# A reordered schedule: lora products paired by batch, gates mixed in eight array tiles

## The chip, the cores and the metric

The kernel runs on one core of a Trainium2 chip. The metric is the time of the device in microseconds (us), as the median of several runs; one further execution is taken by the profiler, and all durations below come from it. The core has a matrix engine TensorE (PE), whose weight loads run beside it (PEld), the vector engine VectorE (DVE), ScalarE (ACT), GpSimd (POOL), and SyncE (SP), which here only issues DMAs. Each engine works off its own queue in order and waits for others through semaphores.

## The reference

```python
# x (64, 64, 1024) is N, C, L; every product is float32
y = conv1d(x, cond_weight, kernel 9, pad 4, 4 groups of 16 channels)
y = y + (cond_128 @ c_weight.T)[:, :, None] + fside_S_0[None, :, None]
# the ffn sees y as 8 batches of 512 rows of 1024
base  = y @ kernel + bias                              # kernel 1024 x 1024
A_eff = einsum('bn,nri->bri', gate, lora_A)            # gate 8 x 16: each batch's mixture
B_eff = einsum('bn,nor->bor', gate, lora_B)            # rank 32
delta = einsum('bor,btr->bto', B_eff, einsum('bri,bti->btr', A_eff, y))
delta = delta + (y @ lora_A_shared.T) @ lora_B_shared.T
out   = x + base + delta
```

## The kernel before

Float32 products are made of three products of rounded parts: each operand is split into a high part (a cast on ACT, steps whose names end in `hi`) and a rest (a subtraction on DVE or POOL, names ending in `lo`), and high times high, high times low and low times high are added in PSUM. The subtraction of step `xlo`, `ylo`, `wlo` and so on runs on DVE where the step ends in `v` and on POOL where it ends in `p`.

The 64 samples are 32 tiles of two; a pair `p` is two such tiles, so there are 16 pairs, and a batch `b` of the ffn is the two pairs 2b and 2b+1. For each pair and each of the four channel groups `g` an input is loaded (`xload`), split, and convolved. For pairs 3 to 15 the convolution is done in a difference form: `xdiff`, `xohi`/`xolo`, `xdhi`/`xdlo`, then `convo` (three matmuls) and `convd` (six); `evmid` and `evac` bring the sums out of PSUM and add the condition, and `turned` transposes the tile into `z`. The 1024 x 1024 product is done by a seven-product scheme (`prod p j`, twelve matmuls each) with sums of input blocks made on POOL (`asum`), splits `yhi`/`ylo`, copies `keep`, and additions `xsum`, `ysum`, `radd`, `yadd`, `total`; pair 0 alone is done plainly (`plain`). The shared lora is folded into the weights at the start (`fmm`, `fadd`).

The lora of each batch works so. `gmask` makes a tile `gm` of gates laid out for a product; `mix w j` multiplies it with raw loads `ls` of lora A (w = 0) and B (w = 1); `mixout` copies the result out of PSUM (ACT), `mixput` writes it to a buffer `eff` in DRAM, and `aload b` and `bload b h` read one batch's part back. `lora p` multiplies A of the batch with pair p's `z` in four tiles of the array of 128 rows by 32 columns; `axlow`, `axsum`, `axhi`, `axlo` add and split the result; `delta p b` multiplies it with B and adds it into the accumulator, and only then `total` may read it.

The order of all work is a text, `ORDER`, a list of about 1,840 steps that was written out beforehand. The program runs the steps in this order, and every engine, queues of DMAs included, keeps it for its own instructions:

```python
    for step in ORDER.replace("\n", " ").split(","):
        if step.strip():
            name, *args = step.split()
            steps[name](*(int(a) if a.isdigit() else a for a in args))
```

So a step's place in the text decides what it waits behind. Accumulators take one of five PSUM banks (`pmm`), convolutions one of two (`pcv`), the lora product has one (`axp`, two halves by p % 2). SP issues the loads and the writes to `eff`; ACT's queue issues the first small loads and the stores. At the start 29 matmuls on a constant tile (`warm`, `busy 29`) run until the first data are there.

Of the kernel before, what the change touches and what calls it, by code (L numbers as in the profile page):

```python
# [10 lines left out]
ALU = mybir.AluOpType  # L11
# [39 lines left out]
small 1, warm, twload 1, busy 29, twload 0, cwload, gload, ctload, cwide, cmul, thi 2, small 0, thi 0, tlo 0 v,  # L51
xload 0 0, xhi 0 0, tlo 2 p, xload 0 1, xlo 0 0 v, conv 0 0, twsum v, xhi 0 1, xlo 0 1 v, conv 0 1, sbload 1,
sbhi 1, csum, evac 0 0 v, turned 0 0, xload 0 2, xhi 0 2, xload 0 3, saload 0, sblo 1 p, xlo 0 2 p, evac 0 1 v,
turned 0 1, saload 1, gmask, xhi 0 3, conv 0 2, xlo 0 3 p, sahi 1, conv 0 3, sahi 0, salo 0 v, fmm 0 1,
sbload 0, sbhi 0, fmm 1 1, wload 1 0, evac 0 2 a, xload 1 0, sblo 0 v, fmm 1 0, salo 1 v, xload 1 1, xhi 1 0,
xhi 1 1, xlo 1 1 p, xlo 1 0 v, turned 0 2, yhi 0 0, ylo 0 0 p, wload 0 1, fadd 0 1, evac 0 3 a, fadd 1 0,
conv 1 0, whi 7 0, fmm 4 0, turned 0 3, xload 1 2, xhi 1 2, wlo 7 0 v, fmm 3 0, wload 1 1, conv 1 1, fadd 1 1,
wload 4 0, fmm 0 0, whi 0 1, wload 0 0, fadd 0 0, evac 1 0 a, plain 0 1 0, fadd 4 0, xlo 1 2 p, turned 1 0,
whi 0 0, wlo 0 1 p, fmm 2 1, fmm 2 0, yhi 0 7, evac 1 1 a, conv 1 2, fmm 5 0, wload 2 1, wload 2 0, fadd 2 0,
wlo 0 0 p, plain 0 0 0, xload 1 3, fadd 2 1, wload 5 0, xhi 1 3, fmm 4 1, xlo 1 3 p, plain 0 0 1, whi 0 2,  # L60
ylo 0 7 v, fadd 5 0, plain 0 3 0, whi 7 1, yhi 0 4, wload 3 0, fadd 3 0, whi 0 3, wload 5 1, fmm 3 1, conv 1 3,
turned 1 1, wlo 7 1 v, wload 3 1, xload 2 0, plain 0 1 1, fadd 3 1, whi 7 2, evac 1 2 v, wlo 7 2 p, wload 4 1,
wlo 0 3 p, wlo 0 2 v, lload 0 6, plain 0 2 0, whi 7 3, plain 0 3 1, fadd 4 1, wload 7 1, turned 1 2, whi 1 1,
plain 0 1 2, lload 0 7, xhi 2 0, plain 0 0 2, ylo 0 4 v, plain 0 3 2, xlo 2 0 v, plain 0 2 1, fmm 5 1,
evac 1 3 a, xload 3 0, wlo 7 3 v, plain 0 2 2, turned 1 3, whi 1 0, yhi 0 1, ylo 0 1 v, fadd 5 1, whi 6 1,
conv 2 0, wload 7 0, thi 1, xdiff 3 0 0 v, wload 6 0, evac 2 0 a, lload 1 5, wlo 1 0 p, fmm 7 0, fadd 7 0,
plain 0 2 3, plain 0 0 3, fmm 6 0, lload 0 2, plain 0 3 3, plain 0 1 3, fadd 6 0, lload 0 5, whi 6 0, asum 1 2,
yhi 1 2, lload 0 0, yhi 1 0, plain 0 0 4, plain 0 2 4, wsum 2 2 v, whi 2 2, lload 1 1, wlo 1 1 p, plain 0 0 5,
fmm 6 1, tlo 1 v, plain 0 2 5, rload 0 2, wlo 6 0 v, wsum 2 1 v, wsum 2 3 v, whi 1 2, wlo 1 2 v, plain 0 1 4,
whi 2 1, asum 1 3, whi 1 3, wlo 1 3 p, xload 2 2, wload 6 1, fadd 6 1, xload 2 1, whi 6 2, lload 0 1, xhi 2 2,  # L70
plain 0 3 4, lload 0 4, plain 0 2 6, lload 1 0, lload 0 3, wsum 2 0 v, fmm 7 1, plain 0 2 7, xload 2 3,
plain 0 0 6, fadd 7 1, whi 6 3, total 0 2, lload 1 6, mix 0 0, mixout 0 0 a, wlo 6 2 v, xhi 2 1, wlo 6 3 v,
wlo 6 1 v, wsum 3 2 v, xlo 2 2 v, mix 0 3, mixout 0 3 a, mix 0 2, mixout 0 2 a, wsum 3 0 v, wsum 5 0 v,
mixput 0 0, whi 2 3, mix 0 1, wsum 3 1 v, mix 1 0, mixput 0 3, mixout 0 1 a, xdiff 3 0 1 p, wsum 4 0 v,
conv 2 2, wlo 2 2 v, whi 2 0, wlo 2 0 v, ylo 1 2 v, plain 0 1 5, wsum 5 1 v, rload 0 0, wsum 5 2 v, wsum 4 2 v,
xlo 2 1 v, plain 0 0 7, mixput 0 1, ylo 1 0 p, mixput 0 2, wlo 2 1 v, prod 1 0, plain 0 1 6, wsum 3 3 v,
wsum 5 3 v, rload 0 1, plain 0 3 5, wsum 4 3 v, bihi, whi 3 2, keep 1 0, plain 0 1 7, lload 1 3, wsum 4 1 v,
plain 0 3 6, mixout 1 0 a, lload 1 7, mix 1 3, aload 0, whi 5 3, yhi 1 3, rload 0 3, lload 1 2, ylo 1 3 v,
mixout 1 3 a, total 0 1, lora 0, mix 1 1, turned 2 0, lora 1, whi 5 0, bilo, xohi 3 0, lload 1 4, mix 1 2,
whi 4 2, wlo 4 2 v, mixout 1 1 a, xolo 3 0 v, whi 3 0, wlo 3 0 v, wlo 3 2 v, yhi 1 1, ylo 1 1 v, mixout 1 2 a,  # L80
asum 1 5, total 0 0, whi 4 1, conv 2 1, axlow 1, axsum 1, xload 3 2, wlo 4 1 p, wlo 2 3 v, whi 4 0,
plain 0 3 7, axlow 0, axsum 0, mixput 1 0, mixput 1 3, wlo 4 0 v, xhi 2 3, xlo 2 3 v, wlo 5 3 v, axhi 1,
prod 1 1, biput 0, axlo 1, whi 3 3, asum 1 6, yhi 1 6, wlo 3 3 v, mixput 1 1, evac 2 1 a, turned 2 1, aload 1,
mixput 1 2, total 0 3, evac 2 2 v, turned 2 2, bload 0 0, whi 3 1, axhi 0, prod 1 2, keep 1 2, conv 2 3,
bhi 0 0, biput 1, yhi 2 0, evac 2 3 a, blo 0 0 v, axlo 0, yhi 1 4, bload 0 1, wlo 3 1 p, prod 1 3, ylo 2 0 v,
delta 0 0 1, total 0 0 1, bhi 0 1, blo 0 1 v, ylo 1 6 p, prod 1 6, whi 4 3, delta 0 3 1, wlo 4 3 v, store 0 0,
ylo 1 4 p, turned 2 3, delta 0 2 1, total 0 3 1, xdhi 3 0, convo 3 0, yhi 1 5, whi 5 1, ylo 1 5 v, xdlo 3 0 v,
delta 1 0, total 0 2 1, xload 3 1, keep 1 3, prod 1 4, evmid 3 0 a, store 0 3, xohi 3 1, xdiff 3 1 0 v,
xdiff 3 1 1 p, wlo 5 1 p, delta 0 1 1, total 0 1 1, wlo 5 0 v, xolo 3 1 p, convd 3 0, evac 3 0, turned 3 0,
asum 2 3, rload 1 0, convo 3 1, yhi 2 1, xdhi 3 1, xdlo 3 1 v, prod 2 0, whi 5 2, store 0 2, delta 1 2,  # L90
xload 3 3, keep 2 0, wlo 5 2 p, yhi 2 3, prod 1 5, total 1 0, xohi 3 3, xolo 3 3 v, asum 2 2, xdiff 3 2 0 p,
store 1 0, convo 3 3, evmid 3 1 a, xdiff 3 2 1 p, convd 3 1, ylo 2 3 v, prod 2 3, rload 1 3, delta 1 1,
ylo 2 1 v, xsum 1, asum 2 5, prod 2 1, xdhi 3 2, evac 3 1, turned 3 1, rload 1 2, radd 1 2 v, xdlo 3 2 v,
xdiff 3 3 0 v, delta 1 3, xohi 3 2, xdiff 3 3 1 p, yhi 2 5, xolo 3 2 v, ylo 2 5 p, yhi 2 2, ylo 2 2 v,
evmid 3 3 a, radd 1 3 v, convo 3 2, total 1 2, store 0 1, evmid 3 2 a, convd 3 2, xdhi 3 3, xdlo 3 3 v,
rload 1 1, radd 1 1 v, bload 1 0, lora 2, axlow 2, asum 2 6, prod 2 2, total 1 1, convd 3 3, evac 3 2,
turned 3 2, axsum 2, xload 4 0, xohi 4 0, xolo 4 0 p, bhi 1 0, yhi 2 4, ylo 2 4 v, axhi 2, prod 2 5, keep 2 3,
yhi 3 0, ysum 1 p, xdiff 4 0 0 v, xdiff 4 0 1 v, prod 2 4, store 1 1, xload 4 1, xohi 4 1, xolo 4 1 p,
yadd 1 v, blo 1 0 v, xdhi 4 0, axlo 2, delta 2 0, yhi 2 6, evac 3 3, keep 2 2, xdlo 4 0 v, convo 4 0,
turned 3 3, convd 4 0, rload 2 0, evmid 4 0 a, total 1 3, total 2 0, ylo 3 0 v, lora 3, xdiff 4 1 0 v,  # L100
xdiff 4 1 1 p, asum 3 3, yhi 3 3, prod 3 0, convo 4 1, ylo 3 3 v, evac 4 0, turned 4 0, xdhi 4 1, xload 4 3,
xohi 4 3, xdlo 4 1 v, asum 3 2, xolo 4 3 v, yhi 3 2, ylo 2 6 v, xload 4 2, xdiff 4 2 0 p, store 1 2,
xdiff 4 2 1 p, xohi 4 2, prod 3 3, yhi 3 1, bload 1 1, evmid 4 1 a, delta 2 2, ylo 3 2 v, xolo 4 2 v, asum 3 5,
store 2 0, convd 4 1, xdhi 4 2, xsum 2, convo 4 2, evmid 4 2 a, evac 4 1, xdlo 4 2 v, rload 2 2, radd 2 2 p,
total 2 2, xdiff 4 3 0 v, xdiff 4 3 1 p, prod 2 6, turned 4 1, yhi 3 4, bhi 1 1, convd 4 2, evac 4 2, keep 3 0,
prod 3 2, ylo 3 1 v, rload 2 3, radd 2 3 v, ysum 2 v, convo 4 3, yadd 2 v, xdhi 4 3, xdlo 4 3 v, ylo 3 4 v,
aload 2, prod 3 1, convd 4 3, turned 4 2, blo 1 1 p, xload 5 0, yhi 3 5, xohi 5 0, keep 3 2, asum 3 6,
keep 3 3, xload 5 1, xohi 5 1, delta 2 3, prod 3 4, delta 2 1, xdiff 5 0 0 p, xdiff 5 0 1 v, axlow 3,
ylo 3 5 p, evmid 4 3 a, total 2 3, prod 3 5, store 2 3, xolo 5 0 p, rload 2 1, yhi 3 6, radd 2 1 p, rload 3 0,
axsum 3, evac 4 3, axhi 3, turned 4 3, yhi 4 0, axlo 3, delta 3 0, xload 5 2, xdhi 5 0, store 1 3, xdlo 5 0 v,  # L110
convd 5 0, convo 5 0, ylo 3 6 v, bload 2 0, ylo 4 0 v, xdiff 5 1 0 v, xdiff 5 1 1 p, total 2 1, prod 3 6,
evmid 5 0 a, prod 4 0, asum 4 3, yhi 4 3, evac 5 0, xsum 3, yhi 4 4, ylo 4 3 p, delta 3 3, delta 3 2,
total 3 0, ylo 4 4 v, lora 4, xolo 5 1 p, xdhi 5 1, xdlo 5 1 v, store 3 0, yhi 4 1, ylo 4 1 v, xohi 5 2,
convo 5 1, keep 4 0, bhi 2 0, prod 4 1, rload 3 3, asum 4 2, yhi 4 2, radd 3 3 v, turned 5 0, xdiff 5 2 0 p,
ysum 3 v, evmid 5 1 a, xdiff 5 2 1 v, ylo 4 2 v, delta 3 1, xolo 5 2 p, rload 3 1, radd 3 1 p, blo 2 0 v,
# [702 lines left out]
```

## Time and profile before

| | before |
|---|---|
| median of 3 runs | 448.08 us (446.77 to 449.16) |
| profiled execution, its time | 447.48 us |
| its span | 445.7 us |
| PE busy | 438.3 us, 98% |
| DVE busy | 391.3 us, 88% |
| ACT busy | 251.2 us, 56% |
| POOL busy | 234.5 us, 53% |
| DMA | 67.05 MB, 150 GB/s on average |

Busy time of an engine is the time in which at least one of its instructions runs; an instruction that overlaps the one before it counts only with what it adds. The chain of waits is followed back from the last instruction, at each step to what released it. A group of the page is all instructions of one source line, engine and operation with the same tiles, with the mean duration of one in ns and the idle time of the engine before them. Matmuls are pipelined, so their durations overlap; start to start is what one costs.

### The profile page before, as it was taken

The numbers are of one execution on the slowest core, as the hardware profiler recorded it, in microseconds if no ns is written. First come the engines' busy times: TensorE is split into PE (matmuls) and PEld (weight loads), VectorE is DVE, ScalarE is ACT, GpSimd is POOL, SyncE is SP. The second block draws the span as 40 slices with busy tenths as digits, with TensorE's granted clock in tenths as the row PEclk, the third lists the DMA queues.
The fourth block names the chain that finished last, engine by engine and source line by source line (L and its number), as shares of the span: only waits on it lengthen the run. The fifth ranks groups of instructions, "written<-read, shape, count | busy, mean of one in ns | idle before, by whom it ended". The sixth has DMA issues, their size and how long they took to land.

```text
span 445.7 us, 7717 instructions
## 1 busy us (share of the span) xinstructions
PE 438.3 (98%) x2557; PEld 358.7 (80%) x2557; DVE 391.3 (88%) x615; ACT 251.2 (56%) x639; POOL 234.5 (53%) x202
## 2 busy tenths in 40 slices
PE   8999999999999999999999999999999999999996
PEld 7677658888888888888878888888888888888884
DVE  5998979899899899889899899899798989887783
ACT  5877468556655566446555655646554745654440
POOL 3766024754747653555444445464656475467543
PEclk9999999999999999999999999999999999999999
DMA  8999582461625463534345453443536354262243
GB/s 229 300 280 308 147 251 66 142 186 49 186 82 158 136 190 110 170 120 136 97 139 147 151 182 91 119 142 90 175 98 186 95 169 151 72 222 90 91 150 118
DMA packets 52488, 67.05 MB, mean 150 GB/s; under 512 B 6112, under 2 KB 34016, under 8 KB 52448
## 3 DMA queue, kind: packets, MB, share of 16 engines
q1 hardware_dynamic: 42512, 49.83, 38.9%
q10 hardware_dynamic: 9936, 16.73, 10.2%
q8 instruction: 20, 0.33, 0.3%
q14 instruction: 20, 0.16, 0.1%
HBM read 47.65 MB, written 18.87 MB: 149 GB/s over the span
## 4 chain that ended last, share of the span: by engine, by line
PE 91%; DMA 4%; DVE 2%; issue 1%; SPq 0%; ACT 0%; ACTq 0%; DVEq 0%
PE mm_a L592 19%; PE mm_d L592 18%; PE mm_c L592 17%; PE mm_b L592 9%; PE cv L346 8%; PE cm L346 4%; PE axp L602 3%; PE cv L318 2%; DMA wr<-in_dram 2%; PE mx L528 2%; PE mm_a L580 1%; PE mm_c L580 1%; DMA ls<-in_dram 1%; DMA ctt<-in_dram 1%; PE mm_d L580 1%; PE mm_a L660 1%
## 5 line engine op out<-in xcount | busy, mean ns | idle before, releaser
L592 PE MATMUL mm_a<-wh,y 128*128 128x512 f32 x240 | 79.6, 392 | 0.0
L592 PE MATMUL mm_d<-wh,y 128*128 128x512 f32 x240 | 79.2, 391 | 0.0
L592 PE MATMUL mm_c<-wh,y 128*128 128x512 f32 x240 | 79.1, 391 | 0.0
L364 ACT ACTIVATE md<-cm,cadd 128x64 f32<-128x64 f32 x208 | 48.2, 315 | 44.8 <-PE cm L346 41.1
L326 POOL TENSOR_TENSOR xf<-xt 128x256 f32<-128x256 f32 x45 | 33.3, 747 | 49.4 <-DVE xd L270 39.4
L265 ACT CAST xd<-xf 128x512 fp32r<-128x512 f32 x52 | 32.5, 626 | 44.9 <-PE cv L346 20.7
L265 ACT CAST y<-s 128x512 fp32r<-128x512 f32 x60 | 37.2, 624 | 30.5 <-POOL s L412 15.3
L592 PEld LDWEIGHTS mm_a<-wh,y 128*128 128x128 f32 x240 | 45.1, 188 | 9.9 <-issue 0.4
L592 PEld LDWEIGHTS mm_d<-wh,y 128*128 128x128 f32 x240 | 45.1, 188 | 9.2 <-issue 0.2
L592 PEld LDWEIGHTS mm_c<-wh,y 128*128 128x128 f32 x240 | 45.1, 188 | 9.1 <-ACT c L636 0.2
L387 DVE STREAM_TRANSPOSE z<-v 128x512 f32<-128x512 f32 x64 | 45.4, 709 | 3.2 <-PE axp L602 1.9
L592 PE MATMUL mm_a<-wl,y 128*128 128x512 f32 x120 | 46.9, 391 | 0.0
L592 PE MATMUL mm_c<-wl,y 128*128 128x512 f32 x120 | 46.8, 390 | 0.0
L592 PE MATMUL mm_d<-wl,y 128*128 128x512 f32 x120 | 46.8, 390 | 0.0
L346 PE MATMUL cv<-xd,th 128*128 128x256 f32 x208 | 45.7, 282 | 0.4 <-DVE xd L270 0.4
L378 DVE TENSOR_TENSOR v<-cv,md 128x512 f32<-128x512 f32 x52 | 35.7, 686 | 7.7 <-PE cv L346 2.5
L270 DVE TENSOR_TENSOR xd<-xf,xd 128x512 fp32r<-128x512 f32 x41 | 34.5, 842 | 7.6 <-ACT xd L265 7.4
L270 DVE TENSOR_TENSOR y<-s,y 128x512 fp32r<-128x512 f32 x49 | 38.2, 782 | 3.0 <-ACT y L265 2.7
L592 PE MATMUL mm_b<-wh,y 128*128 128x512 f32 x120 | 39.6, 391 | 0.0
L346 PEld LDWEIGHTS cv<-xd,th 128*128 128x128 f32 x208 | 35.5, 188 | 2.4 <-DVE xd L270 0.6
L265 ACT CAST y<-z 128x512 fp32r<-128x512 f32 x49 | 30.6, 625 | 11.8 <-DVE c L641 4.5
L326 DVE TENSOR_TENSOR xf<-xt 128x256 f32<-128x256 f32 x59 | 33.7, 587 | 0.2
(132 smaller groups left out, 1008.2 us busy)
## 6 DMA issues: line engine op xcount, KB each, us to landing
xt<-in_dram SPq DMA_DIRECT2D x64, 258.0 KB, 3.2
r<-in_dram SPq DMA_DIRECT2D x64, 256.0 KB, 3.5
out_dram<-r ACTq DMA_DIRECT2D x63, 256.0 KB, 2.6
ls<-in_dram SPq DMA_DIRECT2D x16, 256.0 KB, 4.6
br<-eff SPq DMA_DIRECT2D x48, 64.0 KB, 2.8
wr<-in_dram SPq DMA_DIRECT2D x16, 176.0 KB, 4.2
eff<-ls SPq DMA_DIRECT2D x16, 128.0 KB, 2.7
wr<-in_dram SPq DMA_DIRECT2D x16, 80.0 KB, 3.9
```

The source lines that it names most:

```text
L265: nc.scalar.copy(dst, src)
L270: engs[eng].tensor_tensor(dst, src, f32(hi), ALU.subtract)
L318: nc.tensor.matmul(ps, a[:, 2 * kt, g, :], b[:, :, kt:kt + P], start=(n == 0), stop=(n == 5))
L326: engs[eng].tensor_tensor(xdf[p, g][:, e], m, odd(p, g), ALU.subtract)
L346: nc.tensor.matmul(ps, a[:, w, g, :], b, start=(n == 0), stop=(n == 2))
L364: nc.scalar.activation(t[:, n], cpm[p, g][:, n], ACTF.Identity, bias=c[:, n:n + 1])
L378: nc.vector.tensor_tensor(v.rearrange("p n (i e) -> p e n i", e=2), cps.pop((p, g)), mid.pop((p, g)).unsqueeze(1).to_broadcast([P, 2, 4, H ...
L387: nc.vector.transpose(z[:, :, :, :, gg, :], vs.pop((p, g)).rearrange("p m j -> p (m j)"))
L528: nc.tensor.matmul(mps[w, j][n * e:n * e + n], gm.rearrange("p b i -> p (b i)"), lraw[w, 2 * j + e], start=True, stop=True)
L580: nc.tensor.matmul(acc[p, BLOCKS[b]], m[:, kk, :], n, start=(k == 0 and q == 0), stop=(k == 7 and q == 2))
L592: nc.tensor.matmul(ps, a[:, k, :], b[bb, k], start=s, stop=(k == HK - 1 and q == 2), skip_group_check=not first)
L602: nc.tensor.matmul(axp[q * R:q * R + R, p % 2, :], a[:, k, :], zs[p, hf][:, k, :], start=k < 2, stop=k >= 6)
```

## The change

Three things change. The lora products of the two pairs of a batch are issued one behind the other by a new step `loras b` (for b = 1 to 7; the first batch keeps two single steps). The gates are mixed in tiles of 64 rows by 32 columns of the array, eight at a time, in four calls instead of eight; gate mask, PSUM tiles, `eff` and the DMAs to and from it are laid out to match. And the whole order is written anew, with other choices of engine for some steps and, as the change puts it, with late DMAs allowed for. The number of `mixout` copies, of DMAs and their sizes stays.

The functions, in full:

```diff
-    NC = P // GC
-    eff = [dram.tile([NC, NB * GC, AW], F32, tag=f"eff{w}", name=f"eff{w}") for w in range(2)]
+    HI = GC // 2
+    eff = [dram.tile([4, NB, 2, 2, 2, HI, AW], F32, tag=f"eff{w}", name=f"eff{w}") for w in range(2)]
     gg = const.tile([P, NB], F32, name="gg")
-    gm = const.tile([P, NB, GC], F32, name="gm")
+    gm = const.tile([P, NB, HI], F32, name="gm")
...
     def gmask():
         ident = slot("s", "ident", (P, P))
         make_identity(nc, ident)
-        mask = slot("s", "mask", (P, GC))
-        nc.vector.tensor_reduce(mask, ident.rearrange("p (i n) -> p i n", i=GC), AX.X, ALU.add)
-        nc.vector.tensor_tensor(gm, gg.unsqueeze(2).to_broadcast([P, NB, GC]),
-                                mask.unsqueeze(1).to_broadcast([P, NB, GC]), ALU.mult)
+        mask = slot("s", "mask", (P, HI))
+        nc.vector.tensor_reduce(mask, ident.rearrange("p (r i n) -> p i r n", r=2, i=HI), AX.XY, ALU.add)
+        nc.vector.tensor_tensor(gm, gg.unsqueeze(2).to_broadcast([P, NB, HI]),
+                                mask.unsqueeze(1).to_broadcast([P, NB, HI]), ALU.mult)
...
     def mix(w, j, pool="m"):
         pl, tag = {"m": (pmm, "mm"), "c": (pcv, "cv")}[pool]
-        mps[w, j] = pl.tile([P, 2 * AW], F32, tag=tag, name=f"mx{w}_{j}")
-        n = NB * GC
-        for e in range(2):
-            nc.tensor.matmul(mps[w, j][n * e:n * e + n], gm.rearrange("p b i -> p (b i)"), lraw[w, 2 * j + e],
-                             start=True, stop=True)
+        for r in range(2):
+            mps[w, j, r] = pl.tile([P, 2 * AW], F32, tag=tag, name=f"mx{w}_{j}_{r}")
+        n, m = NB * HI, P // 2
+        for e in range(4):
+            for r in range(2):
+                nc.tensor.matmul(mps[w, j, r][n * e:n * e + n], gm[m * r:m * r + m].rearrange("p b i -> p (b i)"),
+                                 lraw[w, 2 * e + j][m * r:m * r + m], start=True, stop=True)
...
-    def mixput(w, j):
-        n = NB * GC
-        for e in range(2):
-            dst = eff[w].rearrange("c p a -> p c a")[:, 4 * j + 2 * e:4 * j + 2 * e + 2, :]
-            nc.sync.dma_start(dst, mev[w, j][n * e:n * e + n].rearrange("p (c a) -> p c a", c=2))
+    def mixput(w, j, r):
+        for c in range(2):
+            dst = eff[w][:, :, j, c, r].rearrange("e b i a -> (e b) i a")
+            nc.sync.dma_start(dst, mev[w, j, r][:, c * AW:c * AW + AW])
...
+    def loras(b):
+        for p in range(BP * b, BP * b + BP):
+            lora(p)
```

The order, its beginning, one stretch from the middle with a `loras`, and its end:

```diff
-small 1, warm, twload 1, busy 29, twload 0, cwload, gload, ctload, cwide, cmul, thi 2, small 0, thi 0, tlo 0 v,
-xload 0 0, xhi 0 0, tlo 2 p, xload 0 1, xlo 0 0 v, conv 0 0, twsum v, xhi 0 1, xlo 0 1 v, conv 0 1, sbload 1,
...
+gload, sbload 1, cwload, gmask, small 0, sbhi 1, twload 0, warm, twload 1, sblo 1 v, xload 0 0, busy 29, xload 0 1,
+cwide, sbload 0, ctload, cmul, thi 2, saload 0, tlo 2 v, twsum p, xload 0 2, thi 0, tlo 0 v, xhi 0 0, xhi 0 1,
+saload 1, xlo 0 0 v, xload 1 0, xload 0 3, wload 0 0, conv 0 0, xlo 0 1 v, sbhi 0, sblo 0 v, sahi 0, wload 3 0,
...
+yhi 6 6, xsum 6, asum 7 3, keep 6 3, xolo 8 1 p, keep 7 0, keep 6 2, ysum 6 v, xload 8 2, evmid 8 0 a,
+ylo 6 4 v, convd 8 0, bhi 3 1, loras 3, axlow 6, axsum 6, yhi 7 3, ylo 6 6 p, blo 3 1 v, convo 8 1, prod 7 1,
+ylo 7 3 v, xload 8 3, xohi 8 3, axhi 6, asum 7 2, axlo 6, prod 6 6, evac 8 0, xdhi 8 1, xdlo 8 1 p, yhi 7 4,
...
+radd 15 3 v, delta 15 1, yadd 15 v, total 15 3, radd 15 1 v, rload 15 0, delta 15 0, store 15 3, total 15 0,
+store 15 0, rload 15 2, radd 15 2 v, delta 15 2, total 15 2, ylo 15 6 p, prod 15 6, totalh 15 1 1, store 15 2,
+totalh 15 1 0, storeh 15 1 0, storeh 15 1 1
```

Steps that change their engine, over the whole order (the letter at the end of the step): from ACT to DVE 14 of the 52 `evmid` and one `evac`; from POOL to DVE five `radd`, seven `wlo`, five `blo`; from DVE to POOL ten `xdiff`, three `ylo`, two `ysum`, one `yadd`, two `wsum`, one `xdlo`, one `xolo` and two of the first splits.

## The prediction

> **What bounds the kernel now.** I read the busy shares of the page first, then the shares of the chain of waits.
>
> ```profile
> PE 438.3 (98%) x2557; PEld 358.7 (80%) x2557; DVE 391.3 (88%) x615; ACT 251.2 (56%) x639; POOL 234.5 (53%) x202
> PE 91%; DMA 4%; DVE 2%; issue 1%; SPq 0%; ACT 0%; ACTq 0%; DVEq 0%
> ```
>
> TensorE (PE) sets the end; VectorE (DVE) is the only other engine near it. So three things count: how much PE work goes, when PE starts, and whether DVE, ten points behind, still delivers in time. For the first I read the pieces of the chain in order of time around one lora product, and the groups of the two products that change.
>
> ```profile
> 291.88 0.70 PE cv L346 x6
> 292.58 1.01 PE axp L602 x32
> 293.60 2.97 PE mm_a L592 x12
> ...
> L528 PE MATMUL mx<-ls,gm 128*64 128x512 f32 x32 | 9.0, 610 | 0.5 <-DMA ls<-in_dram 0.4
> L602 PE MATMUL axp<-z,ar 128*32 128x128 f32 x512 | 17.3, 276 | 0.0
> ```
>
> To see: a lora product holds PE for 1.01 us, and the product behind it takes 2.97 where its like take 2.72 to 2.76. For the start I read the timeline of the first microseconds and, later on, of the gate tile.
>
> ```profile
> 0.86 0.27 DVE L695 MEMSET axt<- 98x256 f32 x1 [0.86 <-PEq L806]
> 1.18 5.38 PE L701 MATMUL idle<-axt 98*128 98x256 f32 x29 [1.18 <-DVE axt L695]
> 1.67 0.45 ACTq L506 DMA_DIRECT2D gg<-in_dram  x1
> 7.47 0.48 PE L318 MATMUL cv<-xsh,th 128*128 128x512 f32 x1
> ...
> 12.43 0.99 DVE L513 TENSOR_TENSOR gm<-gg,mask 128x64 f32<-128x64 f32 x1
> ```
>
> To see: the 29 idle matmuls start as soon as DVE has written their operand, at 1.18, and end 0.9 us before the first convolution. Last, DVE's busy time in stretches of 25 us, and what it waited for in the first 135 us.
>
> ```profile
> core 0: us, PE busy (x) PEld busy (x) DVE busy (x) ACT busy (x) POOL busy (x), PEclk, DMA share, GB/s
> 0.00:25.00 25.00, 22.54 (x100) 17.35 (x101) 19.86 (x32) 17.61 (x39) 14.00 (x17) 1.00 0.92 264
> 25.00:50.00 25.00, 25.00 (x109) 17.59 (x108) 23.75 (x37) 17.48 (x37) 12.46 (x10) 1.00 0.84 255
> 50.00:75.00 25.00, 24.55 (x157) 17.26 (x156) 21.75 (x39) 15.87 (x37) 6.82 (x5) 1.00 0.63 176
> 75.00:100.00 25.00, 24.99 (x150) 20.77 (x149) 22.15 (x31) 14.37 (x39) 15.59 (x13) 1.00 0.50 156
> 100.00:125.00 25.00, 25.00 (x155) 21.16 (x154) 23.29 (x38) 14.25 (x37) 14.08 (x13) 1.00 0.40 119
> ...
> DVE cwe L727 <- DMA cwt<-in_dram: 3.7, 1, 3.7
> DVE z L387 <- PE axp L602: 1.9, 1, 1.9
> DVE r L666 <- PE dl L660: 1.4, 2, 1.0
> ```
>
> To see: DVE's idle time in the first 125 us is 14.2 us, 5.1 of it before 25 us.
>
> **The change part by part.** Clock of the sum: the profiled execution took 447.48 us (span 445.7); the median of the runs is 448.08, so 0.6 goes on top of what comes out.
>
> *Lora products.* From two runs per batch to one, for batches 1 to 7; batch 0 keeps two. Inside a run the 32 matmuls come as eight groups of four, a group every 0.109 us: 0.87. A run costs 1.01 plus 0.22 on what follows (2.97 less 2.75), so entering and leaving costs 0.36. Seven pairs of switches go: -2.5 us of PE. The trace shows no lora directly behind a lora; if the second had to wait for the first, nothing would be saved, so between 0 and -2.5, and I take -2.5 because groups inside a run pay nothing. What waits longer: every delta of the earlier pair, and with it its accumulators in PSUM (five banks). The order puts one to three products between loras and its first delta (2.7 us each, against about 2.5 for the chain axlow, axsum, axhi, axlo by their rows), so nothing is added, except at most 0.5 at loras 5 and 7, where one product alone covers.
>
> *Gate mix.* Before, 8 calls of two 128x64 tiles; now 4 calls of eight tiles of 64 rows by 32 columns. The eight calls held PE for 8.9 us, of which 1.2 and 0.4 at 57 to 61 us were waits for the ls loads; a clean call is 0.93 (4.67 for five in the chain). A matmul is 0.44 from start to start on its tile and goes in two passes, so eight tiles side by side need 0.9 to 1.0 a call: 4.0 for four, against 7.4. Since each call now stands alone among full-array products, some three more switches at 0.3: net -2.5, and the waits (-1.6) may go or come again. Side by side by columns is shown by the lora row (four tiles start within 0.02 us); by rows nothing is shown. The Trainium skill ("TensorEngine Tiling (Array Packing)", Key Properties and Gotcha 1) says that tiles run independently, but that row tiles must not be in one PSUM bank at once. The code gives the two row halves different banks, so the rule allows -2.5; but a call then takes two of the five banks at once, a cost that the rule names and the old row does not have. If the halves ran one after the other, each call would double: +1.2 instead of -2.5. I take -2.5 and keep +1.2. mixout stays eight ACT copies (0.59 each), mixput 16 DMAs of 128 KB, aload and bload the same count and bytes with rows of 1 KB as before: nothing, covered by the several microseconds between landing and use; without that cover, one 3.3 us load once.
>
> *The head.* gmask now stands before warm in DVE's queue, and its product needs the gate load. That load is now first on ACT's queue, at about 0.74; the load that held this place (bia) landed after 3.3 us and the gate itself took 3.7, so it lands at 4.0 to 4.5. gm took 0.99 beside a POOL operation and half that size now: 0.3 to 0.6. Then the memset, 0.27. So the idle matmuls start at 4.7 to 5.3 instead of 1.18. They cannot be shortened: they run 0.21 us apart in the trace until 4.97, 0.12 after it. By the trace they last 5.4 (full speed 3.8 us after their start); the skill ("TensorE: Matmul & The Clock Gate", What's actually happening) makes the moment depend on a free-running window, which would allow about 5.0 to 6.3. I take 5.4. Convolution 0 0 then starts near 10.9 instead of 7.47: +3.5 (3.0 to 5). ctload now waits behind sbhi 1 on ACT (issue near 4, 4.3 to land: 8.3), which is still ahead of 10. In return the loads are in place by then: before, PE lost 2.4 us from 10 to 20 us (0.9 of it before conv 0 3, on POOL's xlo), and I let those go. Net about +1.1.
>
> *DVE.* Counted over both orders, moves between engines: evmid 14 from ACT to DVE (a 128x256 read of PSUM took 0.41 at cadd), radd 5, wlo 7, blo 5 and one evac to DVE; xdiff 10, ylo 3, ysum 2, yadd 1, wsum 2 and a few small ones to POOL. In all DVE gains 6 us (391 to 397), ACT loses 13, POOL none. ACT and POOL stay far below; what is hidden there stays hidden.
>
> *The order.* I charge each step the time that it adds to its engine's busy time (the charges add up to 391.3 on DVE), and add up what stands ahead of one step in each queue. Take prod 3 6, which needs ylo 3 6. Before: 123.9 us of PE work and 117.9 of DVE work (184 instructions) stand ahead; ylo really ended at 133.8, so DVE had been idle or slower for 15.9, and prod started at 134.9. After: 119.8 of PE, but 126.6 of DVE (199 instructions): seven more wlo, four more xdiff and three more xolo are now ahead of it. In between the surplus of DVE over PE is 4 to 5 us at prod 1 3 and convd 3 1, and 7.7 at convo 5 1, the worst; before it was under 1 from 60 us of PE work on, and soon negative. So from about 70 to 140 us DVE leads and PE waits for it. DVE's idle time there: in the head about 7 (4.0 waiting for the gate, then csum and evac 0 0 wait for the late PE); later, of the 14.7 before 133.8, 4.6 was the start and 4.7 waits on PE, so some 5 remain. ylo 3 6 ends near 126.6 + 12 = 138.6, and prod 3 6 starts there: 3.8 later than before. From there PE needs 301.6 more by the count; before it needed 303.1 and took 306.8 to its end at 441.67. So the end comes at 138.7 + 305.3 = 444.0: +2.3. Further on the surplus shrinks (0 at convd 7 0, DVE 8 behind PE at convd 13 2), so nothing more is added in the middle case. In other words, the 5 us of PE work saved are paid back by the late start and by waits for DVE.
>
> *The rest of the order.* SP issues the same 257 DMAs and ACT the same 69; loads that move ahead in the queue of SP are those of inputs, which wait for nothing; mixput and aload stand behind rload 0 1 as before. The last product, the two half totals and the last stores are the same at the end: 0.
>
> 447.48 + 2.3 = 449.8; with the 0.6 between profile and median, 450.4.
>
> **Rivals.** *DVE keeps up (faster).* If idle time on DVE shrinks to 7 or 8 us before ylo 3 6, PE never waits for it, and the end is the start of conv 0 0 (10.9) plus 420.5 of PE work plus 6 to 7 us of small gaps: 438, or -3.6; with a head that costs less, -5: 443 to 444.5. For it: DVE ran 95% busy from 25 to 50 us already. Against: casts on ACT sit between most DVE pairs.
>
> *DVE leads through the whole run (slower).* At convd 13 2 DVE has 324.0 us ahead instead of 317.1, and in the trace had lost 31.4 by then; if all of that idle time is forced (31.4 plus 2 for the head), xdlo ends at 357.4, PE has 89.2 plus 0.9 to go, and the end is 447.5, +5.8: 454. It decides where forced idle time passes 27 us there.
>
> *Row halves do not overlap.* +3.7 on the middle case: 454.
>
> *The merged lora saves nothing.* +2.5 where PE leads, less where DVE does: 451 to 453.
>
> **How the numbers follow.** Middle case 0.40 (448.5 to 452.5, half of it within the bound), DVE keeps up 0.24, DVE leads all along 0.24, rows or lora fail 0.12. A measurement of this kernel can tell about 0.5% from no change, 2.2 us: faster is below 445.8, slower above 450.3. Faster 0.24; same 0.28; slower 0.48. The range leaves out the outer tenth on each side: 443 to 457.
>
> **What would show it.** Right: the first idle matmul at about 5 us, conv 0 0 near 11; mx matmuls in bursts of eight, about 1 us a call; nine stretches of axp instead of 16, seven of them near 1.9; PE idle or delayed by DVE (xdlo, ylo, evac) between 70 and 140 us, with DVE at 94% or more there. Wrong: idle matmuls still at 1.2 us; PE gapless to 140 us; a mix call near 2 us; or new PE waits for DMA.

## The result, and the profile after

The changed kernel takes 454.16 us (median of 4 runs, 454.08 to 455.02), the kernel before 448.3 us beside it on the same chip (446.77 to 449.16): a ratio of 1.0139, 95% interval 1.0108 to 1.0169. It is slower, as forecast, and inside the range; the forecast was 450.4. The profiled execution took 454.08 us, its span is 452.3.

The busy shares and the shares of the chain of waits, after:

```profile
PE 438.7 (97%) x2589; PEld 358.0 (79%) x2589; DVE 400.7 (89%) x626; ACT 238.8 (53%) x579; POOL 239.7 (53%) x206
PE 79%; DVE 7%; issue 4%; DMA 3%; ACT 3%; POOL 2%; SPq 1%; DVEq 0%; POOLq 0%
```

To see: PE's busy time rose from 438.3 to 438.7 us, although by the prediction's sum the change takes about 5 us of work from it. Something on PE became dearer. The chain shows that the two cheapened parts did become cheaper (start, duration, piece, number of instructions):

```profile
44.96 1.02 PE mx L532 x16
47.57 1.02 PE mx L532 x16
50.89 1.02 PE mx L532 x16
54.92 1.02 PE mx L532 x16
...
156.71 1.88 PE axp L605 x64
158.59 0.91 PE cv L346 x6
159.50 2.80 PE mm_d L595 x12
```

Four mix calls take 4.1 us in place of 8.9, and a paired lora 1.88. The last line is the telling one: a product of twelve matmuls takes 2.80 us; its like took 2.72 to 2.76 before. The groups say the same for all of them. Before (mean ns of one matmul after the comma):

```profile
L592 PE MATMUL mm_a<-wh,y 128*128 128x512 f32 x240 | 79.6, 392 | 0.0
L592 PE MATMUL mm_d<-wh,y 128*128 128x512 f32 x240 | 79.2, 391 | 0.0
L346 PE MATMUL cv<-xd,th 128*128 128x256 f32 x208 | 45.7, 282 | 0.4 <-DVE xd L270 0.4
```

and after:

```profile
L595 PE MATMUL mm_d<-wh,y 128*128 128x512 f32 x240 | 80.6, 396 | 0.1
L595 PE MATMUL mm_a<-wh,y 128*128 128x512 f32 x240 | 80.5, 396 | 0.0
L346 PE MATMUL cv<-xd,th 128*128 128x256 f32 x208 | 45.4, 282 | 0.3 <-DVE v L378 0.3
```

To see: no wait stands beside these groups, and yet the product matmuls are on average 4 to 5 ns longer, while the 256-column convolution is unchanged. Taken from start to start in the trace (stalls left out), a product matmul went from a mean of 228.4 ns (median 227) to 233.5 (232), from the first pair to the last, at a granted clock of 1.00. There are 1,356 of them (1,260 in `prod`, 96 in `plain`): 1,356 x 5.1 ns = 6.9 us. The measured difference is 5.9.

The head and the waits, after: the timeline of the first microseconds, then what PE waited for (us in total, times, longest).

```profile
3.69 0.19 DVE L515 TENSOR_TENSOR gm<-gg,mask 128x32 f32<-128x32 f32 x1 [2.06 <-DMA gg<-in_dram]
3.89 0.27 DVE L702 MEMSET axt<- 98x256 f32 x1
4.21 5.47 PE L708 MATMUL idle<-axt 98*128 98x256 f32 x29 [4.21 <-DVE axt L702]
10.34 0.49 PE L318 MATMUL cv<-xsh,th 128*128 128x512 f32 x1
```

```profile
PE idle L708 <- DVE axt L702: 4.2, 1, 4.2
PE cm L346 <- POOL xo L270: 1.4, 1, 1.4
PE mm_a L667 <- DMA bst<-bih: 1.3, 1, 1.3
PE cm L346 <- DVE md L366: 0.4, 1, 0.4
```

Work in stretches of 25 us, after:

```profile
core 0: us, PE busy (x) PEld busy (x) DVE busy (x) ACT busy (x) POOL busy (x), PEclk, DMA share, GB/s
25.00:50.00 25.00, 24.76 (x128) 17.93 (x127) 24.48 (x39) 16.77 (x38) 12.22 (x8) 1.00 0.96 288
50.00:75.00 25.00, 24.77 (x185) 18.14 (x184) 23.21 (x39) 19.18 (x44) 7.18 (x5) 1.00 0.49 154
75.00:100.00 25.00, 23.73 (x118) 19.53 (x118) 23.83 (x40) 13.08 (x35) 12.61 (x11) 1.00 0.51 149
100.00:125.00 25.00, 24.59 (x178) 20.36 (x177) 24.53 (x40) 14.77 (x36) 13.25 (x11) 1.00 0.36 114
```

DVE is 93 to 98% busy there, and PE loses only 2.2 us in the four rows.

### The profile page after: what moved, and what is told of

The parts are those of the page before. It is cut to its first block, busy times and chain, and to the rows that moved or that the text cites. A ratio compares the mean times of both kernels' runs of the same rounds, so it can differ in the third digit from the quotient of the medians.

```text
span 452.3 us, 7709 instructions
## 1 busy us (share of the span) xinstructions
PE 438.7 (97%) x2589; PEld 358.0 (79%) x2589; DVE 400.7 (89%) x626; ACT 238.8 (53%) x579; POOL 239.7 (53%) x206
## 4 chain that ended last, share of the span: by engine, by line
PE 79%; DVE 7%; issue 4%; DMA 3%; ACT 3%; POOL 2%; SPq 1%; DVEq 0%; POOLq 0%
PE mm_d L595 16%; PE mm_a L595 16%; PE mm_c L595 15%; PE mm_b L595 7%; PE cv L346 7%; PE cm L346 4%; PE cv L318 2%; PE axp L605 2%; DMA wr<-in_dram 2%; DVE y L270 1%; PE mm_d L583 1%; PE mm_b L583 1%; PE idle L708 1%; DVE r L673 1%; POOL xf L326 1%
## 5 line engine op out<-in xcount | busy, mean ns | idle before, releaser
L595 PE MATMUL mm_d<-wh,y 128*128 128x512 f32 x240 | 80.6, 396 | 0.1
L595 PE MATMUL mm_c<-wh,y 128*128 128x512 f32 x240 | 80.4, 396 | 0.0
L326 POOL TENSOR_TENSOR xf<-xt 128x256 f32<-128x256 f32 x55 | 43.4, 801 | 51.3 <-DVE xd L270 50.1
L595 PEld LDWEIGHTS mm_d<-wh,y 128*128 128x128 f32 x240 | 45.1, 188 | 10.9 <-DVE r L673 0.5
L364 ACT ACTIVATE md<-cm,cadd 128x64 f32<-128x64 f32 x152 | 35.4, 317 | 21.6 <-PE cm L346 14.7
L270 DVE TENSOR_TENSOR y<-z,y 128x512 fp32r<-128x512 f32 x39 | 36.7, 940 | 1.4 <-ACT y L265 1.2
L412 POOL TENSOR_TENSOR s<-s,z 128x512 f32<-128x512 f32 x15 | 22.6, 1510 | 24.4 <-ACT xo L265 14.1
```

Source lines behind the costliest of these rows:

```text
L270: engs[eng].tensor_tensor(dst, src, f32(hi), ALU.subtract)
L326: engs[eng].tensor_tensor(xdf[p, g][:, e], m, odd(p, g), ALU.subtract)
L364: nc.scalar.activation(t[:, n], cpm[p, g][:, n], ACTF.Identity, bias=c[:, n:n + 1])
L412: engs[eng].tensor_tensor(t, m, n, op)
L595: nc.tensor.matmul(ps, a[:, k, :], b[bb, k], start=s, stop=(k == HK - 1 and q == 2), skip_group_check=not first)
```

## The experiments

What has no wait in the profile and touches one kind of matmul alone needed another sort of test. In a product matmul the moving operand is a weight piece (`wh`, `wl`; all pieces are buffers of one kind, 2,048 bytes apart) and the stationary one is 128 columns of a half of `y`. The buffers of each kind lie in SBUF in the order in which the steps first use a kind. The new order loads a lora weight (`sbload 1`) near the front, and so the pieces moved from byte 69,440 of a partition to 44,576. The addresses below are those of the compiled programs.

**Shifting all buffers by 32 bytes.** A tile of 32 bytes that nothing uses, in the changed kernel (a_pad32) and in the one before (b_pad32):

```diff
     bih = const.tile([P, NBIAS, 8], F32R, name="bih")
+    pad = const.tile([P, 8], F32, name="pad")
```

> The changed kernel with one unused tile of 32 bytes per partition behind the constants: no instruction is added, and every working tile lies 32 bytes higher, so the weight pieces wh and wl start at a multiple of 64 bytes instead of 32 beside one. Theory A (where the moving operand starts sets the pace of a matmul): start to start of a product's matmul falls from 232 to 227 ns; 1,356 such matmuls give -6.5 to -7 us, so about 447.3. xd moves to a multiple of 64 as well, so convd should fall below 117 ns. Rival B (the order alone costs it: DVE leads and PE waits): 232 ns stays, the time is 453.5 to 455. Rival C (contention of memory accesses with other engines): the pace changes little, under 1 ns.

> The kernel before with the same unused tile of 32 bytes behind the constants; there it takes the weight pieces from a multiple of 64 bytes to 32 beside one. Theory A: product matmuls slow from 227 to 232 ns, +6.5 to +7 us, 454.5 to 455. Rivals B and C: no change, 448.

Measured: a_pad32 454.78 us (ratio to before 1.0149, 1.0129 to 1.0169), product matmuls still 233.6 ns; b_pad32 449.71 (1.0037, 1.0017 to 1.0056), still 229.0. So the place of the pieces on the count of 64 bytes, taken alone, is not the cause. Both shift the pieces and `y` together, which turned out to matter.

**The lora products apart again.** In a_pad32, each `loras b` is split into two lora products, with one PE step of the order between them:

```diff
-loras 3
+lora 6
...
+lora 7
```

> The changed kernel with the 32 byte pad, and each loras taken apart: the earlier pair's product goes one PE step ahead, so a convolution, product or delta stands between the two, for batches 1 to 7. Theory: seven entries into and exits from the tiled mode come back, 0.33 us each, +2.3 us of PE work over the padded kernel where PE leads (449.6 if that one is at 447.3). Rival (the second lora gains nothing behind the first, or DVE hides it): within 0.5 us of the padded kernel.

Measured: 455.93 us (455.03 to 457.39) against 454.78 (454.31 to 455.21) for a_pad32: +1.15 in the medians. In the traces, from the start of prod 3 6 to PE's end, which holds six of the seven pairs, it takes 314.86 us against 312.31: +2.55, of which 0.5 is more idle time on PE. The other 2.1 us agree with 6 x 0.36 = 2.2. Ahead of prod 3 6 the profiled execution of a_split was 1.65 us the quicker one; no run here tells why.

**The head of before.** The first 27 steps as in the old order, the rest of the new one behind them:

```diff
-gload, sbload 1, cwload, gmask, small 0, sbhi 1, twload 0, warm, twload 1, sblo 1 v, xload 0 0, busy 29, ...
+small 1, warm, twload 1, busy 29, twload 0, cwload, gload, ctload, cwide, cmul, thi 2, small 0, ...
```

> The changed kernel with the first 27 steps of the order before (memset and idle matmuls first, filter and input loads ahead of the shared lora's loads), the rest of the new order behind them. Since the convolution's tiles are then used before the first weight piece, the weight pieces lie at a multiple of 64 bytes without a pad. Theory A: 227 ns a matmul, and conv 0 0 starts near 7.5 instead of 10.3; if PE leads in the first 130 us, the 2.9 us of the head come off on top of the 7: 444.5. If DVE leads there (as the prediction has it), most of the head's gain is lost again in waits for DVE: 446.5 to 447.5. If address plays no part: 451 to 454.

Measured: 447.76 us, ratio 1.0 (0.9981 to 1.0018), and product matmuls at 228.4 ns to the end of the run. A head of 10 us sets the pace of the 430 us behind it. Besides the order of 27 steps it changes two things: when PE starts, and where the buffers lie.

**Start or place.** Three kernels take these apart. In a_warm only `warm` moves to the front of the new order; in a_tags the order stays, and buffers of five kinds are set aside ahead of it, by tiles that no instruction uses; in b_wfirst the order of before gets one load moved to its front.

```diff
-gload, sbload 1, cwload, gmask, small 0, sbhi 1, twload 0, warm, twload 1, ...
+warm, gload, sbload 1, cwload, gmask, small 0, sbhi 1, twload 0, twload 1, ...
```

```diff
+    for tag, n, shape in (("r", 4, (P, HN)), ("s", 2, (P, HN)), ("xt", 2, (P, 4, JB)), ("xo", 2, (P, 4, JB)),
+                          ("xd", 1, (P, 2, 4, JB))):
+        for i in range(n):
+            work.tile(list(shape), F32, tag=tag, name=f"{tag}_{i}", bufs=n)
     steps = locals()
```

```diff
-small 1, warm, twload 1, busy 29, ...
+sbload 1, small 1, warm, twload 1, busy 29, ...
```

> The changed kernel with one step moved: warm, DVE's fill of the tile that the idle matmuls read, becomes DVE's first step. The idle matmuls then start near 1.2 us and not at 4.2; every tile lies where it lay in the changed kernel (the weight pieces from byte 44,576 of a partition on). Theory S (the pace of a product matmul is set by how early or evenly TensorE is brought to work in the head): it falls from 232 to 227 ns, TensorE's end falls by about 7 us, total 446 to 449 us. Theory L (the pace is set by where the tiles lie in SBUF): it stays at 232 ns and the total at 453 to 455 us, since conv 0 0 waits for its loads and splits and not for the idle matmuls.

> The changed kernel with its list of steps untouched, but with the buffers of five kinds (r, s, xt, xo, xd) set aside ahead of the list, by tiles that no instruction uses. The weight pieces then lie from byte 69,312 of a partition on, as in the kernel before, and not from 44,576; the idle matmuls start at 4.2 us as in the changed kernel. Theory L (place in SBUF): product matmuls at 227 ns, TensorE's end about 7 us earlier, total 446 to 449 us. Theory S (start of TensorE): 232 ns, total 453 to 455 us. If it is neither (the order of the instructions itself), 232 ns here and in the kernel with the fill moved ahead.

> The kernel before with one step moved: the load of one half of a lora weight (sbload 1), which is the first to use a buffer of the weight pieces, goes to the front of the list. The weight pieces then lie from byte 44,704 of a partition on and not from 69,440, and SP issues one load of 64 rows about 2 us earlier; everything else stands as it was, the idle matmuls start at 1.2 us. Theory L (place in SBUF): product matmuls go from 227 to 232 ns, total 448.3 + 1,356 x 5 ns = about 455 us. Theory S (start of TensorE): 227 ns, total 448 to 449.5 us.

Measured: a_warm 453.96 us (ratio 1.0132, 1.0092 to 1.0173) with the idle matmuls from 1.2 us and 233.5 ns; a_tags 448.81 (0.9999, 0.9985 to 1.0013) with the idle matmuls from 4.1 us and 228.4 ns; b_wfirst 455.1 (1.0157, 1.0129 to 1.0185) at 233.5 ns. The start has no part in the pace; the place has all of it. Groups of a_tags, then of b_wfirst:

```profile
L595 PE MATMUL mm_a<-wh,y 128*128 128x512 f32 x240 | 79.4, 392 | 0.0
L595 PE MATMUL mm_d<-wh,y 128*128 128x512 f32 x240 | 79.4, 392 | 0.1
```

```profile
L595 PE MATMUL mm_a<-wh,y 128*128 128x512 f32 x240 | 80.7, 397 | 0.0
L595 PE MATMUL mm_d<-wh,y 128*128 128x512 f32 x240 | 80.3, 395 | 0.0
```

To see: the changed kernel with old places has the old 392 ns, the old kernel with new places the new 395 to 397.

**Which feature of the place.** In all kernels up to here the quick ones have pieces and `y` alike on the count of 64 bytes, the slow ones 32 apart. An unused buffer of 32 bytes between the two, set aside just ahead of the first use of `y`, moves `y` and no piece; what moves with `y` (`xf`, `md`, one buffer of `xt`, the small lora tiles, and in the changed kernel `v`) is no operand of a product matmul:

```diff
+    def ygap():
+        work.tile([P, 8], F32, tag="gap", name="gap", bufs=1)
...
-xload 1 0
+ygap, xload 1 0
```

> The changed kernel with an unused buffer of 32 bytes set aside ahead of the first use of the y buffers (the step ygap before xload 1 0). No instruction changes; the weight pieces stay at byte 44,576 of a partition (32 on the count of 64) and y0_0 moves from 210,624 (0) to 210,656 (32). Theory R (a product matmul takes 227 ns where its moving operand, a weight piece, and its stationary one, a half of y, lie alike on the count of 64 bytes, and 232 ns where they lie 32 apart; all ten kernels so far agree): 227 ns, the stretch from prod 3 6 to TensorE's end about 307 us and not 312, total 448 to 450 us. Theory P (what counts is where the pieces lie, from about 45 KB on or from about 69 KB on): 232 ns, 453 to 455 us. A wider count (128 bytes and more, on which the two still differ here by 64): 232 ns.

> The kernel before with the same unused buffer of 32 bytes ahead of the first use of y. The weight pieces stay at 69,440 (0 on the count of 64) and y0_0 moves from 212,800 (0) to 212,832 (32); no instruction changes. Theory R (the two operands alike on the count of 64 bytes): product matmuls go from 227 to 232 ns, total 448.3 + 1,356 x 5 ns = about 455 us. Theory P (place of the pieces): 227 ns and 448 to 449.5 us.

Measured: a_ygap 450.58 us (1.0042, 1.0026 to 1.0057), 229.7 ns; b_ygap 453.79 (1.0114, 1.0099 to 1.013), 233.0 ns. Thirty-two bytes that nothing reads or writes make the changed kernel 3.6 us quicker, and the kernel before 5.4 us slower. Groups of a_ygap, then of b_ygap:

```profile
L601 PE MATMUL mm_d<-wh,y 128*128 128x512 f32 x240 | 79.9, 394 | 0.1
```

```profile
L598 PE MATMUL mm_d<-wh,y 128*128 128x512 f32 x240 | 80.4, 396 | 0.0
```

Ten of the fourteen kernels by where their operands lie (bytes from the start of a partition to the first piece and to the `y` that is used first; the rest of each on division by 64; the mean from start to start of a product matmul; the stretch from prod 3 6 to PE's end, which holds 1,020 of the 1,356). The other four fit: a_split lies as a_pad32 does (233.6 ns), best as a_ygap (229.6), and in b_mix (228.5) and a_both (228.4) the distance is 0.

| kernel | pieces | y | rests | distance, rest by 2,048 | ns | stretch, us |
|---|---|---|---|---|---|---|
| before | 69,440 | 212,800 | 0, 0 | 0 | 228.4 | 306.7 |
| b_pad32 | 69,472 | 212,832 | 32, 32 | 0 | 229.0 | 307.3 |
| a_head | 69,312 | 210,624 | 0, 0 | 0 | 228.4 | 308.0 |
| a_tags | 69,312 | 210,624 | 0, 0 | 0 | 228.4 | 307.8 |
| a_ygap | 44,576 | 210,656 | 32, 32 | 160 + 32 | 229.7 | 309.1 |
| after | 44,576 | 210,624 | 32, 0 | 160 | 233.5 | 312.4 |
| a_pad32 | 44,608 | 210,656 | 0, 32 | 160 | 233.6 | 312.3 |
| a_warm | 44,576 | 210,624 | 32, 0 | 160 | 233.5 | 312.4 |
| b_wfirst | 44,704 | 212,800 | 32, 0 | 160 | 233.5 | 311.4 |
| b_ygap | 69,440 | 212,832 | 0, 32 | 32 | 233.0 | 311.3 |

What follows: the two operands of a product matmul should lie alike on the count of 64 bytes; 32 apart costs about 5 ns a matmul. a_ygap gets back 3.8 of the 5.1 ns; in it the two still differ by 64 on the count of 128, or the absolute rest of 32 counts a little, as b_pad32's 0.6 hints. Which of these holds the last nanosecond was not tried.

**The new mix in the old order.** The new functions, the order of before, four mix calls put among the places of the eight; the lora products stay apart:

```diff
-mix 0 0, mixout 0 0 a ... mix 0 2, mixout 0 2 a ... mix 0 1
+mix 0 0, mixout 0 0 0 a, mixout 0 0 1 a ... mix 0 1, mixout 0 1 0 a, mixout 0 1 1 a
```

> The changed kernel's functions under the order of before: the gates mixed in eight tiles of the array (four calls of 1.02 us for eight of 1.11), the two first lora products of a batch still apart. Theory: mixing alone takes 8.9 - 4.1 = 4.8 us off TensorE; all of it lies ahead of prod 3 6, where DVE is busy 93 to 98% and hands out the weight sums, so part is lost in waits: total 444 to 447.5 us. Rival: DVE sets prod 3 6 and the gain is lost there wholly: 447.5 to 449. If the pace of product matmuls moves with the place of the pieces alone, it is 227 ns here, since they lie from 69,312 on.

Measured: 455.75 us (1.0172, 1.0136 to 1.0207), with product matmuls at 228.5 ns: both theories missed. The waits of PE; then, in the kernel before, the load of A that `lora 0` needs and `lora 0` itself; then the same in b_mix; then four stretches of b_mix (length, PE busy, granted clock, DMA share, GB/s):

```profile
PE axp L608 <- DMA ar<-eff: 3.8, 1, 3.8
PE dl L670 <- DVE axt L633: 2.9, 1, 2.9
```

```profile
54.82 0.56 SPq L550 DMA_DIRECT2D ar<-eff  x1
59.36 1.08 PE L602 MATMUL axp<-z,ar 128*32 128x128 f32 x32
```

```profile
54.56 0.66 SPq L556 DMA_DIRECT2D ar<-eff  x1
59.56 1.44 PE L608 MATMUL axp<-z,ar 128*32 128x128 f32 x32 [3.84 <-DMA ar<-eff]
60.94 1.96 PE L535 MATMUL mx<-ls,gm 64*32 64x512 f32 x16
```

```profile
56.00:60.00 4.00, 0.44 (x16) 1.00 0.95 268
60.00:64.00 4.00, 4.00 (x72) 0.57 0.31 103
64.00:70.00 6.00, 6.00 (x48) 1.00 0.42 135
80.00:84.00 4.00, 3.96 (x11) 0.58 0.33 120
```

To see: A's part is asked for at the same time as before (54.6 and 54.8 us) and `lora 0` starts at the same time (59.6 and 59.4). PE comes to it 3.6 us sooner, since the mixing ahead of it takes less, and waits that out; so the gain is lost at that load, and not at DVE as the rival had it. B comes later: a mix call now needs four loads and not two, B's first call stands behind `lora 0`, and its results go to `eff` from 63.6 us on and not from 57.8. The second wait, 2.9 us at a delta, follows a load of B's part that lands at 78.1. Behind each wait the clock is granted at 0.57 to 0.58 over 4 us, and the first lora takes 1.44 us and not 1.01. Prod 3 6 starts 6.0 us later than before. In the new order `lora 0` waits 0.2 us.

**An attempt at a better one.** The changed kernel with the gap, and five moves where its trace shows PE waiting:

```diff
-gload, sbload 1, cwload, gmask, ...
+warm, gload, sbload 1, cwload, gmask, ...
-conv 2 1, biput 1, ...
+conv 2 1, biput 0, biput 1, ...
-prod 2 5, yhi 2 6, convo 4 1, prod 2 4, turned 4 0, ...
+prod 2 5, yhi 2 6, prod 2 4, convo 4 1, turned 4 0, ...
-prod 5 3, convo 6 3, xload 7 2, convd 6 2, radd 4 1 v, prod 5 5, ...
+prod 5 3, xload 7 2, convd 6 2, radd 4 1 v, prod 5 5, convo 6 3, ...
-xolo 8 1 p
+xolo 8 1 v
```

> The changed kernel with the 32-byte gap ahead of y, and four steps of its order moved where its trace shows TensorE waiting: warm first (start of the idle matmuls 4.2 to 1.2 us; conv 0 0 earlier by 0 to 1.5), biput 0 up to biput 1 (delta 1 0 waits 1.5 us for it), xolo 8 1 from POOL to DVE (convo 8 1 waits 1.4 us), convo 4 1 and convo 6 3 each behind one more product (0.65 and 0.96 us). If product matmuls run at 227 ns: 454.2 - 6.8 for the pace - 2.5 to 4.5 for the waits = 443 to 445 us, ratio to before 0.988 to 0.993. Rival: the moved steps make later ones late (convd and evac behind the two moved convo, DVE one more operation): 446 to 448.5. At 232 ns: 450 to 452.

Measured: 451.87 us (1.0081, 1.0059 to 1.0103), at 229.6 ns: no better than the gap alone (450.58), and above both ranges that were given for the quicker pace. The stretch behind prod 3 6 takes 309.5 us, with the gap alone 309.1: there the rival's account holds. The waits of PE in it, then a stretch of the head with the granted clock:

```profile
PE pc L746 <- DMA ctt<-in_dram: 1.9, 1, 1.9
PE cv L349 <- DVE v L381: 1.4, 4, 0.4
PE dl L673 <- POOL bst L273: 1.1, 1, 1.1
```

```profile
10.00:13.00 3.00, 3.00 (x9) 0.50 1.09 304
```

The 1.4 us of convo 8 1 are gone, and 1.4 come back in four waits for evacuations; delta 0 1 1 is late (1.1 us, behind POOL) in place of delta 1 0. In the head the idle matmuls now end at 7.2 us, PE waits 1.9 us for a load, and the clock is granted at 0.50 while conv 0 0 runs. The earlier start has gained nothing: prod 3 6 starts at 135.3 us, with the gap alone at 135.4.

**The two moves that had done something, alone.** Buffers set aside as in a_tags, and `warm` first as in a_warm; nothing else is changed.

> The changed kernel with the two moves that did something, and nothing else: the buffers of r, s, xt, xo and xd set aside ahead of the list (weight pieces at 69,312, y0_0 at 210,624, alike on the count of 64 bytes and of 2,048), and warm first. Theory: product matmuls at 227 ns; idle matmuls from 1.2 us, conv 0 0 at 9.5 to 10.5; prod 3 6 near 134.2 as with warm first alone; 307.8 from there to TensorE's end as with the buffers alone, so an end near 442.0, total 446.5 to 448 us, ratio to before 0.995 to 1.000. Rival: what starts earlier only waits longer at lora 0 or delta 1 0 (DVE sets prod 3 6): total as with the buffers alone, 448.5 to 449.5.

Measured: 448.97 us (446.2 to 452.33 in 22 runs), ratio 1.0007 (0.9988 to 1.0025). In the trace prod 3 6 starts at 132.9 us and PE ends at 440.8, a little earlier than the theory's 134.2 and 442.0, but the profiled execution (446.92) lies below the median. In 12 executions the mean granted clock was 0.997 to 1.000 and the median time 447.5, as the theory says; in the other 10 it was 0.990 to 0.996, and the median 449.4. The kernel before had 0.998 to 1.000 in all 27 of its own beside it. Where in the run the clock was lost is not recorded for these ten; the trace of best, which also has `warm` first, shows such a loss in the head. No version beat the kernel before.

## Why the prediction was right and wrong

Point by point, by the steps of the sum:

- **Lora products:** held. Seven paired stretches of 1.88 us; taking six of them apart gives 2.1 us of PE work back (2.2 by the working). `lora 0` and `lora 1` ran as one stretch too, so there are eight and not nine.
- **Gate mix:** held. The rows of the array do run side by side: 1.02 us a call, just above the 0.9 to 1.0 of the working. (Had they not, the working's own terms give +1.5 and not +1.2.)
- **Head:** the mechanism held, the size was a little too large. `gm` took 0.19 us and not 0.3 to 0.6, the idle matmuls started at 4.21 (4.7 to 5.3) and took 5.47 (5.4), conv 0 0 started at 10.34 (10.9).
- **DVE ahead of prod 3 6:** this step failed. The working had DVE lead from 70 to 140 us and PE wait for it: 126.6 us of DVE work and 12 of idle time ahead of the end of ylo 3 6, at 138.6, and prod 3 6 right behind it. Measured: 123.75 busy and 10.75 idle, the end at 134.5, and prod 3 6 only at 135.6, with PE at work in between. Over the whole run DVE's busy time rose by 9.4 us, not 6. From 70 us to prod 3 6, after:

```profile
70.00:135.60 65.60, 63.92 (x369) 52.88 (x368) 63.19 (x107) 38.87 (x99) 30.47 (x26) 1.00 0.47 145
```

  DVE was as full as said (96%), but PE lost 1.7 us there, and 1.3 of them, at delta 1 0, to a DMA; no more than 0.4 us is put down to DVE. The step "the rest of the order", which put SP's queue at nothing, missed that DMA. A new wait of PE for a DMA was one of the prediction's own signs of being wrong. SP's part of the timeline after:

```profile
71.86 1.92 SPq L559 DMA_DIRECT2D br<-eff  x3
73.82 0.45 SPq L293 DMA_DIRECT2D xt<-in_dram  x1
74.31 0.55 SPq L752 DMA_DIRECT2D bst<-bih  x1
```

  biput 0 (`bst<-bih`) stood behind bload 0 1 (`br<-eff`), for whose destination SP waited 1.5 us, until DVE had done a `wlo`; then it took 3.9 us to land by the chain.

- **From prod 3 6 to PE's end:** this step failed too. The working took 301.6 us of work plus 3.7 that before had lost, 305.3; it took 312.4. It priced every product matmul at before's pace and never asked whether moving first uses could change that. Of the 7.1 us, 1,020 x 5.1 ns = 5.2 are the pace; by a_tags, the same order with operands alike, 4.6 (312.4 less 307.8). The other 2.5 (307.8 less 305.3) are in the main waits that the count did not see (PE is idle there for 0.4 us before and for 2.7 in a_tags), the longest the 1.4 us of convo 8 1 for POOL's xolo.

So the end came at 448.0 and not at 444.0: 3.1 us earlier at prod 3 6 than worked out (with 336 x 5.1 ns = 1.7 us of slower matmuls in it), 7.1 later behind it. The prediction had the change lose 3.8 us ahead of prod 3 6 and win 1.5 back behind it; it lost 0.7 and then 5.6. That the direction and the range came out was luck: two errors of opposite sign. Without the pace the change makes no difference that can be measured (a_tags 0.9999, a_both 1.0007): what lora and mix save goes into the late start and into single waits. PE stood idle for 3.4 us ahead of its end before and for 9.3 after, 3.0 of the difference at the start. The rival in which DVE leads all along (454) came near in time, and by another cause.

## What to carry to other kernels

When one kind of matmul gets longer by the same few ns everywhere and no wait stands beside it, look at where its operands lie before looking at the order: a first use moved in the program can move buffers. Print the addresses of the moving and the stationary tile, and keep them alike on the count of 64 bytes, with a padding buffer or by setting buffers aside up front. A change of functions and of order is judged only after that, and a wait that is removed by hand is worth what the next late thing leaves of it.

## What the runs showed of the hardware

- A 512-column product of rounded float32 parts takes 227 ns from start to start where the distance of its two operands is a multiple of 2,048 bytes, 229 where they lie alike on the count of 64 bytes but 64 apart on that of 128, and 232 where they lie 32 apart (medians; fourteen kernels). The 256-column matmuls of `convd` do not show it: 117.6 ns with the moving operand's buffer 32 bytes off (a_tags) and 117.7 on the count of 64 (a_pad32). Why there is a difference at all, no run here tells.
- Behind a wait of 3.8 us on PE the granted clock was 0.57 over 4 us (b_mix), and the next lora took 1.44 us instead of 1.01: there the wait cost more than its length. The clock was also lost behind waits of 2.9 us (b_mix) and 1.9 us (best), and not behind those of 1.3 and 1.4 us in the changed kernel; what decides it was not tried.
- Eight tiles of 64 rows by 32 columns, the two row halves in two PSUM banks, run side by side: 1.02 us for a call of 16 matmuls (after), where a call of four on tiles of 128 by 64 took 0.93 (before).
